# Distances' operand rows by block transposes and a trip through DRAM, with the aggregation one graph later

## Chip, cores, metric

The kernel runs on one core of a Trainium2 chip. The metric is the device time of one execution in microseconds; the time of record is the median over several runs.

## The reference, cut to what matters

There are 64 graphs of 256 nodes with 256 features. Layer 0 normalises an adjacency matrix and applies it and a weight matrix; a residual and a layer norm follow. Layer 1 has three branches that start from its result `x`: a convolution over the nodes, a message branch with distances, and a gated unit that joins them.

```python
# layer 1, message branch
s    = x @ w_se.T + b_se                       # 3 numbers for each node
sq   = sum(s * s, -1)
dist = sq[:, :, None] + sq[:, None, :] - 2 * einsum('bnd,bmd->bnm', s, s)
A    = exp(-dist) * mask                        # mask: the adjacency matrix given to the kernel's layer
msg  = relu(x @ w_msg.T + b_msg)
x_nmp = einsum('bnm,bmd->bnd', A, msg)          # the aggregation
x_in = concatenate([x_conv, x_nmp], -1)         # the gated unit's input
```

All data and arithmetic are float32.

## The kernel before

**Stages.** The graphs go in four groups of 16 (`Q`). For each group every graph passes `layer0` (from the adjacency matrix to `x1`) and `layer1` (first convolution, distances, messages, aggregation, and a small Fourier transform of the first convolution's output into the tile `V`). When 16 graphs are in `V`, the group's second convolution is done in the frequency domain: `products` multiplies `V` by the weights' transforms `u`, which are loaded from DRAM through six buffers, and `complex_end` transforms back and stores `xc_d`. Then `gates` runs the gated unit graph by graph: it loads what `layer1` stored (`xn_d`), `x1` and `xc_d`, multiplies by `wall` into `p_g`, and writes the output. Stages are overlapped: graphs 0 to 15 run beside the making of the weights' transforms (`weights`, matmuls `p_u`), the next 12 beside the first group's products and back transform, and later graphs beside the gates of the group before.

**Order.** Each stage is a Python generator that stops at `yield`; the functions `graphs`, `paced`, `merge` and `take` say which generator goes on next, and instructions are then put on the engines by a scheduler that may move a ready instruction ahead of one that it expects to wait. Each engine works off its own list strictly in order. SP issues nearly all loads in order, too: while it waits for a buffer or for data, later loads stand behind.

In `graphs` one graph's `layer1` is cut in seven pieces. `PLACES` says after which piece a piece of `layer0` (for two graphs ahead) or of the other work follows; `STATS` and `APPLIED` say where the last parts of a `layer0` (its layer norm's statistics, then the scaling) are taken up:

```python
PLACES = (("other",), ("layer0",), (), (), ("layer0",), ("other", "layer0"), ())
STATS, APPLIED = len(PLACES) - 1, 2
```

**The distances.** `p_conv` (L446) gives 256 features and the three columns of `s` for each chunk of 128 nodes. ScalarE copies the features to `h` and the three columns, four times over, into the constant tile `scols` (L450), where ones and zeros stand already; VectorE adds the halves of the negated squares (L454 to L457). TensorE turns the two chunks of `scols` with the identity (L495, into `p_rows`), ScalarE copies 64 of the rows to `dist_l` (L497) and VectorE the other 64 to `dist_r` (L499). A matmul over 32 rows for each chunk then gives `p_dist` (L506), ScalarE takes its Exp into `aT` (L507), and VectorE multiplies by the adjacency matrix (L508). The aggregation `p_nmp` (L515) follows in the next piece; ScalarE copies its result into `xn` (L519) and issues the store of `xn` to `xn_d` (L520).

The pieces of `layer1` are, in this order: `x1T` (turning `x1`, L429, into `xn`), `p_conv` with the columns, `p_msg`, `p_dft`, `p_rows`, `p_dist` with Exp and product, `p_nmp` with the store. For 12 graphs (`ALONE`) the turning of the next graph's `x1` stands just ahead of `p_nmp`.

**Buffers.** `xn` has two, `msg` and `aT` one each, `dist_l` and `dist_r` one each; `ps` is a pool of four PSUM banks that all of these products share.

Of the kernel before, what the change touches and what calls it, by code (L numbers as in the profile page):

```python
# [9 lines left out]
F32 = mybir.dt.float32  # L10
AF = mybir.ActivationFunctionType
ALU = mybir.AluOpType
AX = mybir.AxisListType

P = 128
# [11 lines left out]
def kernel(  # L27
# [44 lines left out]
    const = ctx.enter_context(tc.tile_pool(name="const", bufs=1))  # L72
    dram = ctx.enter_context(tc.tile_pool(name="dram", bufs=1, space=bass.MemoryType.DRAM))
# [4 lines left out]
    work = ctx.enter_context(tc.tile_pool(name="work", bufs=2))  # L78
# [3 lines left out]
    def bank(name):  # L82
        return ps.tile([P, 512], F32, tag="bank", name=name)
# [7 lines left out]
    def mark(op, gates=0):  # L91
        marks.append((op.ins, gates))
# [43 lines left out]
    ident = const.tile([P, P], F32)  # L136
# [8 lines left out]
    nc.vector.tensor_scalar(alpha_t, alpha_t, MIN_ALPHA, None, op0=ALU.max)  # L145


    scols = const.tile([P, NCH, P], F32, name="scols")
    nc.gpsimd.memset(scols, 0.0)
    for c in (NSE, 32 + NSE):  # L150
        nc.gpsimd.memset(scols[:, :, c : c + 1], 1.0)

# [187 lines left out]
    xn_d = [dram.tile([P, 2 * DCH, N], F32, name=f"xn_d{g}") for g in range(B)]  # L340
    XN = {}
    ALONE = set()
# [80 lines left out]
    def x1_transposed(g):  # L423
        x1 = X1.pop(g)
        xn = XN[g] = work.tile([P, 2 * DCH, N], F32, name="xn")
        p = bank("p_x1T").rearrange("p (k n) -> p k n", k=DCH)
        for k in range(DCH):
            for c in range(NCH):
                nc.tensor.transpose(p[:, k, c * P : (c + 1) * P], x1[:, c, k * P : (k + 1) * P], ident)  # L429
        nc.vector.tensor_scalar(xn[:, 0], p[:, 0], others_only, unit, op0=ALU.mult, op1=ALU.add)  # L430
        nc.scalar.copy(xn[:, 2 * DCH - 1], p[:, 1])

    def layer1(g, place):

        if g not in XN:
            x1_transposed(g)
        xn, adjT = XN.pop(g), ADJT.pop(g)
        x1T = xn[:, 0 : 2 * DCH : 2 * DCH - 1]
        yield

        h = work.tile([P, NCH, D], F32, name="h", bufs=1)
        cols = scols.rearrange("p c (q r) -> p c q r", r=32)
        for c in range(NCH):
            p = bank("p_conv1")[:, : D + NSE]
            for k in range(DCH):
                nc.tensor.matmul(  # L446
                    p, x1T[:, k, c * P : (c + 1) * P], wc1[:, k, :], start=k == 0, stop=k == DCH - 1
                )
            nc.scalar.activation(h[:, c, :], p[:, :D], AF.Relu)
            nc.scalar.copy(cols[:, c, :, :NSE], p[:, D:].unsqueeze(1).to_broadcast([P, 4, NSE]))  # L450

        s3 = cols[:, :, 0, :NSE]
        sq3 = small.tile([P, NCH, NSE], F32, name="sq3")
        nc.vector.scalar_tensor_tensor(sq3, s3, -1.0, s3, op0=ALU.mult, op1=ALU.mult)  # L454
        nsq = small.tile([P, NCH], F32, name="nsq")
        nc.vector.tensor_reduce(nsq, sq3, AX.X, ALU.add)
        last = nc.vector.tensor_scalar(  # L457
            cols[:, :, 2:4, NSE], nsq.unsqueeze(2).to_broadcast([P, NCH, 2]), 0.5, None, op0=ALU.mult
        )
        mark(last)  # L460
        mark(last)
        yield
        msg = work.tile([P, NCH, D], F32, name="msg", bufs=1)
        p = bank("p_msg").rearrange("p (c d) -> p c d", c=NCH)
        for c in range(NCH):
            for k in range(DCH):
                nc.tensor.matmul(  # L467
                    p[:, c, :], x1T[:, k, c * P : (c + 1) * P], wmsg[:, k, :], start=k == 0, stop=k == DCH - 1
                )
        mark(nc.scalar.activation(msg, p, AF.Relu))  # L470
        yield


        mid = GT // 2
        if TILES[0] is not V:
            AWAY.append(place)
        for k in range(DCH):
            p = bank("p_dft")

            for c, t0, t1 in ((0, 0, mid + 1), (1, mid - 1, GT)):  # L480
                first = t0 + 1 - c * mid
                nc.tensor.matmul(  # L482
                    p[:, t0 * FL : t1 * FL], h[:, c, k * P : (k + 1) * P],
                    fwd[:, first : first + t1 - t0, :].rearrange("p t f -> p (t f)"),
                    start=c == 0, stop=True, skip_group_check=c == 1,
                )
            nc.scalar.copy(
                TILES[0][:, :, k, place * GT : (place + 1) * GT],
                p[:, : GT * FL].rearrange("p (t f) -> p f t", f=FL),
            )  # L490

        yield
        p = bank("p_rows")
        for c in range(NCH):
            nc.tensor.transpose(p[:, c * P : (c + 1) * P], scols[:, c, :], ident)  # L495
        dl = work.tile([64, N], F32, name="dist_l", bufs=1)
        nc.scalar.copy(dl, p[0:64, :N])  # L497
        dr = work.tile([64, N], F32, name="dist_r", bufs=1)
        nc.vector.tensor_copy(dr, p[64:P, :N])  # L499
        yield  # L500

        aT = work.tile([P, NCH, 2, P], F32, name="aT", bufs=1)
        for c in range(NCH):
            rows = slice(32 * c, 32 * c + 32)
            p = bank("p_dist")[:, :N]
            nc.tensor.matmul(p, dl[rows, c * P : (c + 1) * P], dr[rows, :], start=True, stop=True)  # L506
            nc.scalar.activation(aT[:, c].rearrange("p n q -> p (n q)"), p, AF.Exp, bias=nsq[:, c : c + 1], scale=2.0)  # L507
        mark(nc.vector.tensor_mul(aT, aT, adjT[:, :, 0:3:2, :]))  # L508
        yield
        if g in ALONE:  # L510
            x1_transposed(g + 1)
        p = bank("p_nmp").rearrange("p (k n) -> p k n", k=DCH)
        for k in range(DCH):
            for mc in range(NCH):
                nc.tensor.matmul(  # L515
                    p[:, k, :], msg[:, mc, k * P : (k + 1) * P], aT[:, mc].rearrange("p n q -> p (n q)"),
                    start=mc == 0, stop=mc == NCH - 1,
                )
        nc.scalar.copy(xn[:, 1 : 1 + DCH], p)  # L519
        nc.scalar.dma_start(xn_d[g], xn)  # L520
        yield

# [412 lines left out]
    def chain(*stages):  # L935
        for stage in stages:
            yield from stage
# [13 lines left out]
    def run(stage):  # L951
        for _ in stage:
            pass
# [14 lines left out]
            yield  # L968


    PLACES = (("other",), ("layer0",), (), (), ("layer0",), ("other", "layer0"), ())
    STATS, APPLIED = len(PLACES) - 1, 2
    ENDS = [iter(())]

    def graphs(first, part, others):


        for i in part:
            load(first + i + 3)
# [12 lines left out]

    with tc.tile_pool(name="setup", bufs=1) as setup:
        load_taps(setup, 0)
# [85 lines left out]
    def copies(V2):  # L1080

        waiting = list(AWAY)
        AWAY.clear()
        TILES[0] = V
        for i in waiting:
            nc.scalar.copy(V[:, :, :, i * GT : (i + 1) * GT], V2[:, :, :, i * GT : (i + 1) * GT])
            yield

    late = nothing()
    for q in range(NQ):  # L1090
        first = (q + 1) * Q
        more = q + 1 < NQ
        end = chain(complex_end(q), copies(V2) if more else iter(()))
# [99 lines left out]
```

## Time and profile before

| | |
|---|---|
| median of 3 runs | 2127.64 us (2127.56 to 2128.44) |
| profiled execution | 2127.71 us, of which span 2125.9 us |
| mean granted TensorE clock | 0.988 |
| TensorE busy (matmuls) | 2006.1 us, 94% of the span |
| VectorE, ScalarE, GpSimd busy | 1474.1, 905.3, 666.8 us |
| DMA | 298.05 MB, mean 140 GB/s |
| `p_rows`: 128 transposes | 24.7 us busy |
| copies to `dist_l` (ScalarE) and `dist_r` (VectorE), 64 each | 23.4 and 27.2 us busy |
| `p_dist`: 256 passes | 46.2 us busy |
| `p_nmp`: 512 passes | 122.6 us busy |

How to read it: times are of one execution on the chip. A float32 matmul is recorded as two passes. Matmuls are pipelined and the recorded lengths overlap, so busy times are more than what an instruction holds back the next one by. PE is TensorE's matmuls, PEld its weight loads, DVE VectorE, ACT ScalarE, POOL GpSimd, SP the engine that only issues transfers. The span is the time from the first to the last instruction; the execution is 1.8 us longer.

### The profile page before, as it was taken

What the parts mean: (1) busy time and instruction counts of PE and PEld (TensorE: products, weight loads), DVE (VectorE), ACT (ScalarE), POOL (GpSimd) and SP (SyncE); (2) the same over time, 40 slices, a digit from 0 to 9 for tenths busy, and PEclk for the clock granted to TensorE, in tenths of its full rate; (3) what the DMA queues carried; (4) which work ended last, traced back from release to release, by engine and by line L of the source; (5) the groups of instructions that cost most, each with busy time, mean ns of one, the idle gap of its engine ahead of it and who ended that gap; (6) DMA issues with size and microseconds to landing.
All of it is one profiled execution on the core that took longest, in us unless ns stands there. A gap on an engine that the chain in (4) does not pass through costs nothing. (4 is left out here: it accounts for less than half of the span.)

```text
span 2125.9 us, 26260 instructions
## 1 busy us (share of the span) xinstructions
PE 2006.1 (94%) x8157; PEld 1443.2 (68%) x8157; DVE 1474.1 (69%) x3347; ACT 905.3 (43%) x2114; POOL 666.8 (31%) x672
## 2 busy tenths in 40 slices
PE   6999999888999999999999999999999999899997
PEld 5888788766667756667777666667777765555554
DVE  5555567775558788774556888875445889977776
ACT  4666643456432234555553123446554123233333
POOL 3445310121431243223321234323232123344443
PEclk9999999999999999999999999999999999999999
DMA  4766556433437645344335655334323754443331
GB/s 125 230 210 200 192 183 209 154 132 119 122 96 226 194 123 139 114 120 120 94 99 179 201 155 140 118 104 134 96 93 100 243 146 131 111 118 95 93 94 56
DMA packets 305289, 298.05 MB, mean 140 GB/s; under 512 B 84192, under 2 KB 283956, under 8 KB 305150
## 3 DMA queue, kind: packets, MB, share of 16 engines
q1 hardware_dynamic: 245198, 200.37, 32.1%
q10 hardware_dynamic: 44480, 67.39, 8.9%
q0 software_dynamic: 15472, 28.61, 6.0%
q8 instruction: 66, 1.08, 0.2%
q14 instruction: 73, 0.60, 0.1%
HBM read 193.19 MB, written 103.06 MB: 139 GB/s over the span
## 5 line engine op out<-in xcount | busy, mean ns | idle before, releaser
L856 PE MATMUL p_g<-wall,sums 128*128 128x384 f32 x1536 | 537.7, 489 | 11.6 <-DVE G L882 11.6
L856 PE MATMUL p_g<-wall,inputs 128*128 128x384 f32 x1152 | 409.4, 492 | 14.5 <-DVE G L874 14.1
L856 PEld LDWEIGHTS p_g<-wall,sums 128*128 128x128 f32 x1536 | 284.6, 191 | 200.3 <-issue 19.1
L856 PEld LDWEIGHTS p_g<-wall,inputs 128*128 128x128 f32 x1152 | 218.5, 192 | 167.5 <-DVE G L874 23.4
L838 POOL TENSOR_TENSOR sums<-inputs 128x384 f32<-128x384 f32 x128 | 139.9, 1093 | 343.2 <-PE p_g L856 296.9
L369 POOL TENSOR_TENSOR dis<-deg,neg_half 128x2 f32<-128x2 f32 x64 | 48.3, 754 | 475.7 <-DVE deg L367 468.6
L897 ACT ACTIVATE G<-G 128x512 f32<-128x512 f32 x128 | 80.7, 630 | 250.8 <-DVE G L884 148.6
L328 POOL TENSOR_TENSOR ln_rs<-ln_rs,neg_half 128x2 f32<-128x2 f32 x129 | 94.9, 736 | 275.1 <-DVE ln_rs L327 226.7
L541 PE MATMUL p_k<-u,VM 128*128 128x256 f32 x736 | 175.8, 381 | 4.1 <-DMA u<-ud 4.1
L541 PEld LDWEIGHTS p_k<-u,VM 128*128 128x128 f32 x736 | 139.4, 191 | 31.3 <-DMA u<-ud 3.9
L446 PE MATMUL p_conv<-wc,xn 128*128 128x259 f32 x512 | 130.4, 392 | 22.7 <-DVE xn L430 21.5
L399 PE MATMUL p_hT<-adjT,x 128*128 128x256 f32 x512 | 126.7, 391 | 15.6 <-ACT msg L470 8.2
L333 ACT ACTIVATE x_g<-x_g,ln_mr,ln_rs 128x256 f32<-128x256 f32 x128 | 70.0, 593 | 150.3 <-DVE ln_mr L331 148.3
L446 PEld LDWEIGHTS p_conv<-wc,xn 128*128 128x128 f32 x512 | 94.2, 191 | 53.1 <-DVE xn L430 31.1
L508 DVE TENSOR_TENSOR aT<-aT,adjT 128x512 f32<-128x512 f32 x64 | 44.8, 699 | 123.0 <-ACT aT L507 122.8
L409 PE MATMUL p_out<-w,hT 128*128 128x256 f32 x512 | 123.7, 384 | 3.4 <-ACT hT L404 3.0
L482 PE MATMUL p_dft<-fwd,h 128*128 128x240 f32 x512 | 117.4, 372 | 9.2 <-ACT scols L450 8.8
L515 PE MATMUL p_nmp<-aT,msg 128*128 128x256 f32 x512 | 122.6, 383 | 0.7 <-DVE aT L508 0.7
L467 PE MATMUL p_msg<-wmsg,xn 128*128 128x256 f32 x512 | 122.0, 381 | 0.0
L838 POOL TENSOR_TENSOR sums<-inputs,sums 128x384 f32<-128x384 f32 x64 | 70.2, 1097 | 161.3 <-PE p_g L856 160.6
L331 DVE SCALAR_TENSOR_TENSOR ln_mr<-ln_mv,ln_rs 128x2 f32<-128x2 f32 x129 | 47.3, 368 | 101.7 <-POOL ln_rs L328 101.7
L409 PEld LDWEIGHTS p_out<-w,hT 128*128 128x128 f32 x512 | 95.6, 190 | 29.9 <-ACT hT L404 9.9
(160 smaller groups left out, 3642.0 us busy)
## 6 DMA issues: line engine op xcount, KB each, us to landing
u<-ud SPq DMA_DIRECT2D x284, 256.0 KB
xn_d<-xn ACTq DMA_DIRECT2D x64, 512.0 KB
inputs<-xn_d SPq DMA_DIRECT2D x64, 512.0 KB
ud<-u_set POOLq DMA_DIRECT2D x39, 480.0 KB, 6.3
adj_t<-in_adj_dram SPq DMA_DIRECT2D x64, 256.0 KB
x_t<-in_x_dram SPq DMA_DIRECT2D x64, 256.0 KB
x_d<-x ACTq DMA_DIRECT2D x64, 256.0 KB
xc_d<-VM SPq DMA_DIRECT2D x64, 256.0 KB
```

The costliest lines, as they stand in the source:

```text
L328: nc.gpsimd.tensor_tensor(rs[:, : len(chunks)], rs[:, : len(chunks)], neg_half[:, : len(chunks)], op=ALU.pow)
L333: nc.scalar.activation(y[:, c, :], y[:, c, :], AF.Identity, bias=mr[:, c : c + 1], scale=rs[:, c : c + 1])
L399: nc.tensor.matmul(p[:, k, :], x1[:, mc, k * P : (k + 1) * P], adjT[:, mc, 1 - mc : 3 - mc, :].rearrange("p n q -> p (n q)"), start=mc == ...
L409: nc.tensor.matmul(p[:, c, :], hT[:, k, c * P : (c + 1) * P], w0[:, k, :], start=k == 0, stop=k == DCH - 1)
L446: nc.tensor.matmul(p, x1T[:, k, c * P : (c + 1) * P], wc1[:, k, :], start=k == 0, stop=k == DCH - 1)
L467: nc.tensor.matmul(p[:, c, :], x1T[:, k, c * P : (c + 1) * P], wmsg[:, k, :], start=k == 0, stop=k == DCH - 1)
L482: nc.tensor.matmul(p[:, t0 * FL : t1 * FL], h[:, c, k * P : (k + 1) * P], fwd[:, first : first + t1 - t0, :].rearrange("p t f -> p (t f)") ...
L515: nc.tensor.matmul(p[:, k, :], msg[:, mc, k * P : (k + 1) * P], aT[:, mc].rearrange("p n q -> p (n q)"), start=mc == 0, stop=mc == NCH - 1,)
L541: nc.tensor.matmul(p[:, j * D : (j + 1) * D], v[:, k, :], u[:, k, :], start=k == 0, stop=k == DCH - 1)
L838: nc.gpsimd.tensor_tensor(S[i], x, y, op=op)
L856: nc.tensor.matmul(p[:, : 3 * HD] if k == 0 else p[:, HD:], a[:, k], wall[:, b, k].rearrange("p t d -> p (t d)"), start=first and k == 0, ...
L897: nc.scalar.activation(rz, rz, AF.Tanh, scale=0.5)
```

## The change

`scols` shrinks from 128 to 32 columns a chunk and holds two groups of four (three columns of `s` and one more) instead of four groups of 32. VectorE turns it in blocks of 32x32 into a new tile `tr`. SP stores `tr` to one of four small DRAM tensors `sd`, and loads from there, with four transfers, the four rows of each chunk that the distances need: `dist_r` with all 256 nodes (in an order by blocks) and `dist_l` with the chunk's 128. TensorE's two transposes, `p_rows` and both copies out of it are gone. The distance matmuls take four rows instead of 32, and the Exp reads PSUM in the blocks' order.

The aggregation leaves the end of its own graph: the graph's tiles are put in `PENDING`, and `aggregated()` runs one graph later, between `p_conv` and `p_msg`, and once more at the end of each run of `graphs`. In the 12 graphs alone, the turning of the next graph's `x1` now stands ahead of `p_dist`. `PLACES`, `STATS` and `APPLIED` are set to the new pieces.

```diff
-    scols = const.tile([P, NCH, P], F32, name="scols")
+    RB4 = NSE + 1
+    scols = const.tile([P, NCH, 32], F32, name="scols")
     nc.gpsimd.memset(scols, 0.0)
-    for c in (NSE, 32 + NSE):
-        nc.gpsimd.memset(scols[:, :, c : c + 1], 1.0)
+    nc.gpsimd.memset(scols[:, :, NSE : NSE + 1], 1.0)
+    sd = [dram.tile([P, NCH * 32], F32, name=f"sd{i}") for i in range(4)]
...
-        cols = scols.rearrange("p c (q r) -> p c q r", r=32)
+        cols = scols[:, :, : 2 * RB4].rearrange("p c (q r) -> p c q r", r=RB4)
...
-            nc.scalar.copy(cols[:, c, :, :NSE], p[:, D:].unsqueeze(1).to_broadcast([P, 4, NSE]))
+            nc.scalar.copy(cols[:, c, :, :NSE], p[:, D:].unsqueeze(1).to_broadcast([P, 2, NSE]))
...
-        last = nc.vector.tensor_scalar(
-            cols[:, :, 2:4, NSE], nsq.unsqueeze(2).to_broadcast([P, NCH, 2]), 0.5, None, op0=ALU.mult
-        )
+        nc.vector.tensor_scalar(cols[:, :, 1, NSE], nsq, 0.5, None, op0=ALU.mult)
+        tr = work.tile([P, NCH * 32], F32, name="tr")
+        last = nc.vector.transpose(tr, scols.rearrange("p c i -> p (c i)"))
+        dl = work.tile([64, P], F32, name="dist_l")
+        dr = work.tile([64, N], F32, name="dist_r")
+        nc.sync.dma_start(sd[g % 4], tr)
+        across = sd[g % 4].rearrange("(b r) x -> r b x", r=32)
+        for c in range(NCH):
+            rows = slice(32 * c, 32 * c + RB4)
+            nc.sync.dma_start(dr[rows].rearrange("r (b x) -> r b x", b=4), across[RB4 : 2 * RB4])
+            nc.sync.dma_start(dl[rows].rearrange("r (b x) -> r b x", b=4), across[:RB4, :, 32 * c : 32 * c + 32])
         mark(last)
         mark(last)
+        yield
+        aggregated()
         yield
...
-        p = bank("p_rows")
-        for c in range(NCH):
-            nc.tensor.transpose(p[:, c * P : (c + 1) * P], scols[:, c, :], ident)
-        dl = work.tile([64, N], F32, name="dist_l", bufs=1)
-        nc.scalar.copy(dl, p[0:64, :N])
-        dr = work.tile([64, N], F32, name="dist_r", bufs=1)
-        nc.vector.tensor_copy(dr, p[64:P, :N])
-        yield
-
+        yield
+
+        if g in ALONE:
+            x1_transposed(g + 1)
         aT = work.tile([P, NCH, 2, P], F32, name="aT", bufs=1)
         for c in range(NCH):
-            rows = slice(32 * c, 32 * c + 32)
+            rows = slice(32 * c, 32 * c + RB4)
             p = bank("p_dist")[:, :N]
-            nc.tensor.matmul(p, dl[rows, c * P : (c + 1) * P], dr[rows, :], start=True, stop=True)
-            nc.scalar.activation(aT[:, c].rearrange("p n q -> p (n q)"), p, AF.Exp, bias=nsq[:, c : c + 1], scale=2.0)
+            nc.tensor.matmul(p, dl[rows], dr[rows], start=True, stop=True)
+            nc.scalar.activation(
+                aT[:, c].rearrange("p n (b i) -> p n b i", i=32), p.rearrange("p (b n i) -> p n b i", n=NCH, i=32),
+                AF.Exp, bias=nsq[:, c : c + 1], scale=2.0,
+            )
         mark(nc.vector.tensor_mul(aT, aT, adjT[:, :, 0:3:2, :]))
-        yield
-        if g in ALONE:
-            x1_transposed(g + 1)
-        p = bank("p_nmp").rearrange("p (k n) -> p k n", k=DCH)
-        ...
-        nc.scalar.copy(xn[:, 1 : 1 + DCH], p)
-        nc.scalar.dma_start(xn_d[g], xn)
-        yield
+        PENDING.append((g, xn, msg, aT))
+        yield
+
+    def aggregated():
+        while PENDING:
+            g, xn, msg, aT = PENDING.pop()
+            p = bank("p_nmp").rearrange("p (k n) -> p k n", k=DCH)
+            ...
+            nc.scalar.copy(xn[:, 1 : 1 + DCH], p)
+            nc.scalar.dma_start(xn_d[g], xn)
...
-    PLACES = (("other",), ("layer0",), (), (), ("layer0",), ("other", "layer0"), ())
-    STATS, APPLIED = len(PLACES) - 1, 2
+    PLACES = (("other",), ("layer0",), (), (), (), ("layer0",), ("other", "layer0"))
+    STATS, APPLIED = 1, 3
     ENDS = [iter(())]
...
             for piece, _ in enumerate(layer1(first + i, i)):
-                if piece == APPLIED:
-                    run(ENDS.pop())
-                    ENDS.append(given["layer0"])
-                elif piece == STATS:
-                    next(given["layer0"], "end")
+                if piece == STATS:
+                    next(ENDS[0], "end")
+                elif piece == APPLIED:
+                    run(ENDS[0])
+                    ENDS[0] = given["layer0"]
...
             yield from given["other"]
+        aggregated()
```

The statistics of a `layer0` are so taken up in the next graph's second piece, where before they came in the last piece of the same graph.

More of the change, by code (lines that the diff above doesn't have):

```diff
@@ L492, in layer1 @@
         yield
-        p = bank("p_rows")
-        for c in range(NCH):
-            nc.tensor.transpose(p[:, c * P : (c + 1) * P], scols[:, c, :], ident)
-        dl = work.tile([64, N], F32, name="dist_l", bufs=1)
-        nc.scalar.copy(dl, p[0:64, :N])
-        dr = work.tile([64, N], F32, name="dist_r", bufs=1)
-        nc.vector.tensor_copy(dr, p[64:P, :N])
-        yield
-        aT = work.tile([P, NCH, 2, P], F32, name="aT", bufs=1)
-        for c in range(NCH):
-            rows = slice(32 * c, 32 * c + 32)
-            p = bank("p_dist")[:, :N]
-            nc.tensor.matmul(p, dl[rows, c * P : (c + 1) * P], dr[rows, :], start=True, stop=True)
-            nc.scalar.activation(aT[:, c].rearrange("p n q -> p (n q)"), p, AF.Exp, bias=nsq[:, c : c + 1], scale=2.0)
-        mark(nc.vector.tensor_mul(aT, aT, adjT[:, :, 0:3:2, :]))
         yield
@@ L511, in layer1 @@
             x1_transposed(g + 1)
-        p = bank("p_nmp").rearrange("p (k n) -> p k n", k=DCH)
[L513 to L518, printed above, removed]
-        nc.scalar.copy(xn[:, 1 : 1 + DCH], p)
-        nc.scalar.dma_start(xn_d[g], xn)
-        yield
+        aT = work.tile([P, NCH, 2, P], F32, name="aT", bufs=1)
+        for c in range(NCH):
+            rows = slice(32 * c, 32 * c + RB4)
+            p = bank("p_dist")[:, :N]
+            nc.tensor.matmul(p, dl[rows], dr[rows], start=True, stop=True)
[3 more added lines that the diff above has]
+            )
+        mark(nc.vector.tensor_mul(aT, aT, adjT[:, :, 0:3:2, :]))
+        PENDING.append((g, xn, msg, aT))
+        yield
+    PENDING = []
+    def aggregated():
+        while PENDING:
+            g, xn, msg, aT = PENDING.pop()
+            p = bank("p_nmp").rearrange("p (k n) -> p k n", k=DCH)
+            for k in range(DCH):
+                for mc in range(NCH):
+                    nc.tensor.matmul(
+                        p[:, k, :], msg[:, mc, k * P : (k + 1) * P], aT[:, mc].rearrange("p n q -> p (n q)"),
+                        start=mc == 0, stop=mc == NCH - 1,
+                    )
+            nc.scalar.copy(xn[:, 1 : 1 + DCH], p)
+            nc.scalar.dma_start(xn_d[g], xn)
     VM = freq.tile([P, FL, D], F32, name="VM")
```

## The prediction

> **What bounds the kernel now.** I read the page's busy times first, then busy time by stage, then TensorE's order in time, then its waits.
>
> The busy line, and three 50 us stages (columns: stage, length, busy us of PE, PEld, DVE, ACT, POOL with instruction counts, granted clock, DMA share, GB/s):
>
> ```profile
> PE 2006.1 (94%) x8157; PEld 1443.2 (68%) x8157; DVE 1474.1 (69%) x3347; ACT 905.3 (43%) x2114; POOL 666.8 (31%) x672
> ```
> ```profile
> 130.00:180.00 50.00, 50.00 (x251) 42.26 (x250) 27.06 (x65) 32.51 (x83) 24.73 (x25) 1.00 0.63 205
> 450.00:500.00 50.00, 42.88 (x210) 34.13 (x210) 38.73 (x108) 27.08 (x74) 9.07 (x9) 1.00 0.30 102
> 1000.00:1050.00 50.00, 48.59 (x213) 36.28 (x212) 25.53 (x71) 26.09 (x66) 17.55 (x18) 1.00 0.41 126
> ```
>
> TensorE is the bound. In the first stage (graphs 0 to 12 beside the weights' transforms, 80 to 230 us) it is never idle; in the stage of graphs alone (450 to 500) it lacks 7 us in 50, and with gates mixed in 1 to 3. So a PE instruction removed is worth its time in the first stage, and a new wait of PE costs its length there.
>
> TensorE's order in time (start, length, instruction):
>
> ```profile
> 167.04 1.78 PE L482 MATMUL p_dft<-fwd,h 128*128 128x240 f32 x8
> 168.66 0.38 PE L495 MATMUL p_rows<-ident,scols 128*128 128x128 f32 x2
> 168.88 1.89 PE L399 MATMUL p_hT<-adjT,x 128*128 128x256 f32 x8
> 170.70 0.70 PE L506 MATMUL p_dist<-dist_r,dist_l 32*128 32x256 f32 x4
> 171.33 1.99 PE L307 MATMUL p_u<-taps,dft_w 85*120 85x256 f32 x8
> ```
>
> The lengths overlap; the price is from start to start. The two transposes of `p_rows` cost 168.88 - 168.66 = 0.22 us, not the 0.38 shown. In the same way eight passes of 256 columns (four matmuls) cost 1.73 (`p_msg`, 165.31 to 167.04), `p_dft` 1.62, four transposes 0.44 (160.96 to 161.40), `p_dist` 0.63, and three matmuls of `p_g` 1.94.
>
> TensorE's waits that touch the edit (us in total, times, longest):
>
> ```profile
> PE p_conv L446 <- DVE xn L430: 21.5, 19, 3.1
> PE p_dist L506 <- DVE dist_r L499: 4.1, 8, 1.1
> PE p_rows L495 <- DVE ln_mv L326: 3.2, 2, 1.6
> PE p_rows L495 <- DVE scols L457: 2.7, 4, 0.9
> PE p_rows L495 <- ACT x L333: 0.5, 1, 0.5
> PE p_hT L399 <- ACT dist_l L497: 1.3, 2, 0.6
> ```
>
> **What goes.** Transposes: 64 x 0.22 = 14.1 us of PE. The waits of `p_rows`, of `p_dist` for `dist_r`, and of `p_hT` for `dist_l`: 3.2 + 2.7 + 0.5 + 4.1 + 1.3 = 11.8 us. The copy on ACT (64 x 0.366 = 23.4) and on VectorE (64 x 0.426 = 27.2) go too; I count nothing for them, since neither is the bound. The new block transpose takes VectorE some of that back: the trace's transpose of 128x512 took 702 ns and its smallest operations about 160, so 128x64 lies between 0.16 and 0.70; I take 0.2, near the small end because it has an eighth of the elements.
>
> **What stays.** `p_dist` keeps its 256 columns; four rows instead of 32 shorten nothing that a row shows. Its two halves are parted by other matmuls in 46 of the 64 graphs in the new order. Four passes of 128 rows cost half of 1.73, 0.87, against 0.63 here, so the parting costs 0 to 46 x 0.24 = 11 us; I take 0. The Exp of 128x256 reads PSUM in runs of 32; copies with equally broken views (L487) cost no more per element than plain ones, so 0.
>
> **The moved aggregation.** Eight passes of `p_nmp`, ACT's copy (0.58 us) and the issue of the 512 KB store of `xn` (0.34) go from the end of graph g to just behind `p_conv` of graph g + 1. `p_nmp` waited 0.7 us in all for its operand, so nothing is won there; the work is moved into the stretch that must now cover the transfers. On ACT the copy stands ahead of the ReLU of `msg`, with 1.7 us of `p_msg` to cover it. The store frees `xn` a graph later: issued about 3 us behind `p_conv`, 3.5 us long in the chain, it is in by about 6.5, and the next write of that buffer comes no earlier than about 7.9 where `x1T` is early; 1.4 us to spare, cost 0. In the stage of graphs alone, `x1T` now stands ahead of `p_dist` and `p_out` (0.63 + 1.73 us) instead of ahead of `p_nmp` (1.73), and VectorE takes `xn` before `p_out`'s epilogue. Of the 21.5 us of `p_conv` waits, some 17 lie between 200 and 640 us; bounds 0 and 17, I take 8.
>
> **The new wait.** `p_dist` now needs: VectorE's chain after `p_conv`, the block transpose, a store, and loads issued only when the store has landed. The first part is in the trace:
>
> ```profile
> 163.12 1.92 PE L446 MATMUL p_conv<-wc,xn 128*128 128x259 f32 x8
> ...
> 167.09 0.17 DVE L457 TENSOR_SCALAR scols<-nsq 128x4 f32<-128x4 f32 x1
> ```
>
> That is 2.2 us from the end of `p_conv` (165.04) to the end of L457 (167.26). Over the 64 graphs this distance X was 1.08 at best, 2.2 in the median, over 3 in 20 of them. For one transfer the nearest rows are small loads:
>
> ```profile
> 2007.59 0.55 SPq L790 DMA_DIRECT2D inputs<-x_d  x1
> 2010.43 1.67 POOL L813 TENSOR_TENSOR inputs<-inputs 128x512 f32<-128x512 f32 x1 [3.19 <-DMA inputs<-x_d]
> ```
> ```profile
> wc<-in_b_se_dram POOLq DMA_DIRECT2D x1, 0.0 KB, 2.4
> wmsg<-in_b_msg_dram POOLq DMA_DIRECT2D x1, 1.0 KB, 2.1
> ```
>
> The first is 2.8 us from issue to user, with 0.55 of issue for 256 pieces; SP's small issues took about 0.28 (0.28 and 0.25 at 2.18 and 2.50 us of the span). So a hop costs 2.1 to 3.4 (the slowest L790 case, 1518.0 to 1521.4); I take 2.4, nearest to the small pieces. Then the operands of the first `p_dist` are there X + 0.3 + 2.4 + 2.4 + 0.28 = X + 5.4 after `p_conv`, those of the second 0.56 later.
>
> Against it stands the cover on PE in the new order: `p_adjT` 0.44, `p_nmp` 1.73, `p_msg` 1.73, `p_dft` 1.62, `p_hT` 1.73 = 7.25 us; `x1T` adds 0.44 where graphs run alone, each `p_u` 0.43, each `p_g` matmul 0.65. Cover is 7.25 or less in 22 graphs, up to 8 in 12, 8 to 8.6 in 17, more in 13. Taking each graph's X against its own cover (for graph 28 without the 6.1 us that `p_dft` itself waits), the waits sum over 64 graphs to 10 us at 2.1 a hop, 19 at 2.4, 32 at 2.7, 58 at 3.0 and 101 at 3.4. I take 19; 15 of it falls in graphs 28 to 63, where X is uneven.
>
> In the first stage three stores of 480 KB a graph (median landing 6.3 us) go out just when the new store does, at a DMA share of 0.6 to 0.75. Two hops that share engines with them may each be a us slower: 13 graphs, 0 to 2.5 us each, 0 to 32; I take 4, since `p_u` lengthens the cover there to 8.5.
>
> A page of the Trainium skill speaks against this change: DMA: Bandwidth & Descriptors, section "Anatomy of one DMA", says that a transfer of any size pays a nearly constant 2 us, most of it the receipt from the memory written, DRAM's being the longest. By it a hop is an estimated 2.1 us and the sum would be about 10 us lower than mine; the 2.8 us row is slower than the rule.
>
> **SP's queue.** Five issues of about 0.28 us a graph, and two waits in order: for the transpose, then for the store's landing. Behind them stand loads of `adj`, `x`, the gates' inputs, stores of `xc` and the loads of `u`. The first four are wanted a graph later. Loads of `u` are six deep (5.2 us of products); in graphs 16 to 19 the new order puts the store behind loads that themselves wait for products after `p_conv`, so SP would stand there anyway. 0 to 3 us in each of four graphs; I take 0.
>
> **Sum.** -14.1 - 11.8 - 8 + 19 + 4 = -11 us. The profiled execution took 2127.71 (span 2125.9), the median is 2127.64, so no correction: 2117 us.
>
> **Rivals.**
> - **Slow hops** (slower). If a hop under load costs 3.0 or more, PE waits 58 us or more, and 2127.7 - 34 + 58 + 10 = 2162. It decides from about 2.7 a hop, where 32 cancels the gain. For: the L790 rows of 2.8 to 3.4, the DMA share, loads queued ahead of the small ones. Against: those rows hold 0.55 us of issue and 256 scattered words. Chance 0.34.
> - **Gain swallowed.** Where PE idles anyway, freed PE time turns into the next wait (`G` for `p_g`, 25.7 us in all); only the first 16 graphs gain 16 x 0.22 = 3.5, and the new waits eat it: 2122 to 2131. For: PE lacks 7 us in 50 in the middle stage. Against: the gates' stages are 97% busy. Chance 0.14.
> - **SP held**: `u` late by 3 us in four graphs on top of the forecast's waits at 2.7 a hop: about 2138. Chance 0.04.
> - **Forecast**, hops of 2.1 to 2.6: 2094 to 2123. Chance 0.48.
>
> **The numbers.** A measurement here tells about 0.2% from no change, 4.3 us. Faster: 0.45 of the forecast's 0.48 and 0.05 of the swallowed gain, 0.50. Same: 0.03 + 0.03 of slow hops near the balance + 0.07 = 0.13. Slower: 0.31 + 0.02 + 0.04 = 0.37. The range, 2098 to 2162, reaches from all `p_conv` waits gone with hops of 2.1 up to hops of 3.0; the forecast case alone is 2098 to 2123.
>
> **What would show it.** Right: no `p_rows`; `p_dist` waiting for DMA `dist_r` or `dist_l` about 20 us in all, mostly behind 500 us; `p_conv` waits for `xn` falling below 15. Wrong: `p_dist` waits of 50 us or more, or spread over the first 230 us (then the stores of `ud` are the reason), or `p_k` waiting for `u` well over its 5.1 us.

## The result, and the profile after

| | before | after |
|---|---|---|
| median | 2128.04 us (2127.56 to 2129.88, 4 runs) | 2278.44 us (2267.23 to 2294.82, 4 runs) |
| profiled execution | 2127.71 us, span 2125.9 | 2279.28 us, span 2277.2 |
| mean granted TensorE clock | 0.988 | 0.954 |

The ratio is 1.0711, 95% interval 1.0645 to 1.0777: 7% slower, where 2117 us was forecast and 2162 was the upper end.

The page's busy line of the changed kernel, then three 50 us stages at about the places of those shown of before (columns as there; the eighth group is the granted clock):

```profile
PE 2092.4 (92%) x8029; PEld 1483.3 (65%) x8029; DVE 1444.1 (63%) x3347; ACT 897.5 (39%) x2050; POOL 663.8 (29%) x671
```
```profile
130.00:180.00 50.00, 42.00 (x177) 32.49 (x175) 16.69 (x40) 23.02 (x55) 14.26 (x14) 0.90 0.49 142
550.00:600.00 50.00, 44.42 (x208) 36.34 (x207) 36.05 (x120) 26.81 (x73) 9.82 (x10) 0.97 0.35 114
1110.00:1160.00 50.00, 46.75 (x183) 34.03 (x182) 19.94 (x60) 25.46 (x63) 12.04 (x13) 0.92 0.36 108
```

TensorE has 128 instructions fewer and is busy 86.3 us longer; its idle time grew from 119.8 to 184.8 us (span less busy). The 151.3 us of the span are these two parts, 86.3 + 65.0. The longer busy time has two parts of its own: a lower clock, and `p_dist`. Its two halves now stand apart, with other matmuls between them, in 46 of the 64 graphs (2 before), and its busy time went from 46.2 to 90.2 us. A graph at full clock and without a wait shows the price of that:

```profile
1084.85 0.69 PE L512 MATMUL p_dist<-dist_r,dist_l 4*128 4x256 f32 x2
1085.48 0.91 PE L870 MATMUL p_g<-wall,sums 128*128 128x384 f32 x2
1086.32 0.69 PE L512 MATMUL p_dist<-dist_r,dist_l 4*128 4x256 f32 x2
1086.94 1.99 PE L410 MATMUL p_out<-w,hT 128*128 128x256 f32 x8
```

From start to start each half costs 0.63 and 0.62 us; together they cost 0.63 before (170.70 to 171.33). An estimate from these rows is 46 x 0.62 = 28 us at full clock for the 46 graphs.

The stage from 30 us to the first product of the first group, before and after, shows the idle time and the lower clock at their largest:

```profile
30.00:282.70 252.70, 245.28 (x1204) 204.65 (x1205) 135.18 (x330) 155.84 (x406) 105.58 (x99) 0.99 0.61 192
```
```profile
30.00:383.60 353.60, 295.98 (x1154) 228.20 (x1154) 130.42 (x326) 154.83 (x384) 104.94 (x99) 0.84 0.48 139
```

Idle time went from 7.4 to 57.6 us there, busy time from 245.28 to 295.98, the clock from 0.99 to 0.84. Of the added busy time, 17.7 us are `p_dist`'s (11.2 before, 28.9 after, partly at the lower clock).

TensorE's waits after (us in total, times, longest), whole span and then 30 to 383 us alone:

```profile
PE p_dist L512 <- DMA dist_l<-sd: 60.2, 30, 5.8
PE p_conv L447 <- DVE xn L431: 17.5, 8, 3.0
PE p_hT L400 <- DVE tr L460: 5.1, 2, 2.6
PE p_k L555 <- DMA u<-ud: 3.9, 4, 1.6
```
```profile
PE p_dist L512 <- DMA dist_l<-sd: 38.1, 11, 5.8
```

The new wait is 60.2 us, 38.1 of it in the first stage. Another 5.3 us there are one wait of `p_u` at 49.5 us, which the kernel before doesn't have. Graph 6 shows what one such wait is made of (start, length, instruction; rows of VectorE, GpSimd, SP and TensorE picked from the timeline):

```profile
167.16 1.99 PE L447 MATMUL p_conv<-wc,xn 128*128 128x259 f32 x8
...
168.57 2.92 POOL L314 TENSOR_TENSOR u_set<-u_set,u_set 120x1024 f32<-120x1024 f32 x1
...
172.11 0.59 POOL L316 DMA_DIRECT2D ud<-u_set  x1
172.19 0.16 DVE L332 SCALAR_TENSOR_TENSOR ln_mr<-ln_mv,ln_rs 128x2 f32<-128x2 f32 x1 [2.92 <-POOL ln_rs L329]
172.27 1.76 DVE L455 SCALAR_TENSOR_TENSOR sq<-scols 128x6 f32<-128x6 f32 x1
...
174.50 0.25 DVE L460 STREAM_TRANSPOSE tr<-scols 128x64 f32<-128x64 f32 x1
```
```profile
174.77 0.36 SPq L463 DMA_DIRECT2D sd<-tr  x1
175.24 1.12 SPq L108 DMA_DIRECT2D adj_t<-in_adj_dram  x1
176.41 2.59 SPq L291 DMA_DIRECT2D taps<-in_conv2T_dram  x1
180.24 0.27 SPq L467 DMA_DIRECT2D dist_r<-sd  x1
```
```profile
182.63 1.19 PE L512 MATMUL p_dist<-dist_r,dist_l 4*128 4x256 f32 x2 [4.24 <-DMA dist_l<-sd]
183.74 2.06 PE L308 MATMUL p_u<-taps,dft_w 85*120 85x256 f32 x4
185.73 1.22 PE L512 MATMUL p_dist<-dist_r,dist_l 4*128 4x256 f32 x2
186.88 3.78 PE L410 MATMUL p_out<-w,hT 128*128 128x256 f32 x8
```

`p_conv` ends at 169.1. VectorE is ready with the block transpose only at 174.75, 5.6 us later: it waits 2.92 us for a small GpSimd operation behind the sum of `u_set`, and soon after L455 takes 1.76 us (the like operation of before 0.17 in the median). The store goes out at 174.77 while two stores of `ud` run, and the first load only at 180.24, 5.5 us later: SP spends 3.7 us of that on issuing two other loads, and then still waits 1.2 us for the store's landing. The loads are quick: the first `p_dist` starts 2.1 us after the issue of the second one, which it needs. It starts at 182.6, 13.5 us after `p_conv`. And then `p_out` lasts 3.78 us, not its usual 1.99. The windows around it say why (same columns):

```profile
177.00:182.00 5.00, 1.38 (x7) 0.84 (x5) 0.00 (x0) 1.17 (x2) 0.00 (x0) 1.00 0.80 246
182.00:187.00 5.00, 4.37 (x9) 2.24 (x9) 0.00 (x0) 1.07 (x3) 0.52 (x1) 0.53 0.23 61
187.00:192.00 5.00, 5.00 (x14) 4.07 (x15) 1.94 (x4) 1.37 (x5) 0.00 (x0) 0.50 0.34 93
192.00:197.00 5.00, 5.00 (x25) 4.23 (x25) 2.47 (x9) 3.03 (x9) 3.61 (x2) 0.94 0.25 57
```

After 4.24 us without work TensorE runs at half its clock. In half-microsecond windows the clock stands at 0.50 from 182.5 to 192.5, ten us in which five us of work are lost. So one wait is paid about twice. Graphs 5 to 10 all look like this and take 23 to 27 us each, where before took 16.

### The profile page after: what moved, and what is told of

It is laid out like the page before. It is cut to its first block, busy times and chain, and to the rows that moved or that the text cites. A ratio compares the mean times of both kernels' runs of the same rounds, so it can differ in the third digit from the quotient of the medians.

```text
span 2277.2 us, 26624 instructions
## 1 busy us (share of the span) xinstructions
PE 2092.4 (92%) x8029; PEld 1483.3 (65%) x8029; DVE 1444.1 (63%) x3347; ACT 897.5 (39%) x2050; POOL 663.8 (29%) x671
## 3 DMA queue, kind: packets, MB, share of 16 engines
q1 hardware_dynamic: 259534, 203.26, 30.7%
## 4 chain that ended last, share of the span: by engine, by line
PE 38%; DVE 21%; DMA 5%; issue 5%; POOL 3%; ACT 3%; SPq 1%; ACTq 0%; POOLq 0%; DVEq 0%
PE p_g L870 22%; PE p_k L555 5%; PE p_out L410 3%; PE p_dist L512 2%; PE p_hT L400 2%; DMA sd<-tr 1%; DMA dist_l<-sd 1%; DVE ln_st L326 1%; POOL ln_rs L329 1%; DVE VM L742 1%; PE p_nmp L530 1%; DVE VM L605 1%; PE p_dft L493 1%; DVE VM L606 1%; DVE G L923 1%
## 5 line engine op out<-in xcount | busy, mean ns | idle before, releaser
L870 PE MATMUL p_g<-wall,sums 128*128 128x384 f32 x1536 | 546.1, 493 | 13.4 <-DVE G L896 13.3
L870 PE MATMUL p_g<-wall,inputs 128*128 128x384 f32 x1152 | 418.0, 498 | 24.5 <-DVE G L888 19.6
L870 PEld LDWEIGHTS p_g<-wall,inputs 128*128 128x128 f32 x1152 | 219.3, 194 | 180.0 <-DVE G L888 30.7
L410 PE MATMUL p_out<-w,hT 128*128 128x256 f32 x512 | 152.4, 450 | 0.7 <-ACT hT L405 0.7
L512 PE MATMUL p_dist<-dist_r,dist_l 4*128 4x256 f32 x256 | 90.2, 478 | 63.2 <-DMA dist_l<-sd 60.2
L410 PEld LDWEIGHTS p_out<-w,hT 128*128 128x128 f32 x512 | 111.9, 225 | 40.6 <-issue 12.3
L400 PEld LDWEIGHTS p_hT<-adjT,x 128*128 128x128 f32 x512 | 99.4, 198 | 44.1 <-ACT x L392 6.4
```

Source lines behind the costliest of these rows:

```text
L400: nc.tensor.matmul(p[:, k, :], x1[:, mc, k * P : (k + 1) * P], adjT[:, mc, 1 - mc : 3 - mc, :].rearrange("p n q -> p (n q)"), start=mc == ...
L410: nc.tensor.matmul(p[:, c, :], hT[:, k, c * P : (c + 1) * P], w0[:, k, :], start=k == 0, stop=k == DCH - 1)
L512: nc.tensor.matmul(p, dl[rows], dr[rows], start=True, stop=True)
L870: nc.tensor.matmul(p[:, : 3 * HD] if k == 0 else p[:, HD:], a[:, k], wall[:, b, k].rearrange("p t d -> p (t d)"), start=first and k == 0, ...
```

## The experiments

The theory at the start: the trip through DRAM arrives too late, TensorE idles, and the idling costs clock on top. Its rivals: the new order costs by itself; SP's extra transfers cost whoever waits for them; the clock falls for another reason; the operands are late for VectorE's sake and not for the transfers'.

To compare kernels by stage I took from each trace the time at which VectorE completes `scols` for a graph, and subtracted that of before. Gain or loss of each stretch in us (the last column is the difference of the whole span):

| kernel | to graph 15 | 15 to 27 | 27 to 32 | 32 to 63 | rest | span |
|---|---|---|---|---|---|---|
| after | +103.3 | -8.7 | +11.6 | +43.4 | +1.6 | +151.3 |
| 1 order alone | +18.5 | -6.9 | +2.9 | -5.4 | -1.0 | +8.1 |
| 2 trip alone | +74.1 | +2.2 | +10.9 | +18.4 | +0.9 | +106.4 |
| 3 no dependence | +31.7 | -10.9 | +0.7 | -10.8 | -4.7 | +6.0 |
| 4 one `ud` store | +47.6 | -7.9 | +7.2 | +34.2 | -2.6 | +78.4 |
| 5 matmuls in the wait | +92.2 | -8.0 | +10.0 | +44.3 | +3.3 | +141.7 |
| 6 distances later | +40.2 | -6.3 | +9.2 | -16.6 | 0.0 | +26.5 |
| 8 mixed | +3.0 | -9.3 | +9.4 | -13.9 | +3.5 | -7.3 |

The graphs with a parted `p_dist`, and its busy time, differ too: 46 and 90.2 us in after, 0 and 46.0 in 1, 39 and 84.0 in 2, 10 and 55.5 in 3, 46 and 82.2 in 4, 43 and 81.7 in 5, 15 and 57.0 in 6, 3 and 46.9 in 8. No experiment changes the parting by itself.

The runs of the kernel before had medians of 2128.0 to 2130.1 us beside these kernels; ratios are to the runs on the same chip.

**1. The order alone.** After's pieces and later aggregation, with the transposes on TensorE put back in the piece that the trip left empty.

```diff
+        p = bank("p_rows")
+        for c in range(NCH):
+            nc.tensor.transpose(p[:, c * P : (c + 1) * P], scols[:, c, :], ident)
...
-        nc.sync.dma_start(sd[g % 4], tr)
...
```

> The aggregation one graph later and the new pieces as in the changed kernel, but the operand rows still by TensorE's two transposes (no trip through DRAM). Theory A (the trip's waits, and TensorE's clock falling behind them, are the whole loss): no wait of p_dist for a DMA, granted clock 0.98 or more, 2110 to 2130 us. Rival B (the new order itself costs in the gates' stages, where 56 us of the loss lies): 2150 to 2190 us. Rival C (the order gains what the prediction claimed, about 8 us of p_conv's waits): 2115 to 2122 us, graphs alone 4 to 8 us shorter.

Measured: 2140.76 us, ratio 1.0042 (1.0025 to 1.0059), clock 0.987. The loss of 150 us isn't in the order. The order costs 18.5 us in the first stage and wins 6.9 among the graphs alone; B falls, C holds only there, and A's total is missed by 11 us, since A gave the order no price.

**2. The trip alone.** The order of before, with the transposes replaced by the trip.

> The trip through DRAM as in the changed kernel, but the aggregation and the pieces as before, so that p_nmp (1.73 us) does not lie between p_conv and p_dist. Theory A: the waits grow by up to 1.7 us a graph and the clock falls further: 2350 to 2450 us, granted clock 0.92 or less. Rival B (the later aggregation costs, not the trip): under 2250 us.

Measured: 2234.59 us, ratio 1.0477 (1.0451 to 1.0503). My expectation missed: I had looked only at the cover, which is 1.73 us shorter, and this kernel is 44 us faster than the whole change. B's number is met, but the trip by itself still costs 106 us. In its first stage `p_dist` waits only 8.0 us for transfers; `p_conv` waits 15.0 for `xn`, `p_nmp` 6.7 for `aT` and `p_u` 5.4 for `taps`, so that pricing `p_dist`'s wait alone misses most of the trip's cost there. In its trace the block transpose ends 2.16 us after `p_conv` in graphs 1 to 12 (4.14 in after), and the store takes 2.70 us until SP issues the first load (4.64 in after). The later aggregation bought 1.73 us of cover and lost more: in its order VectorE's chain comes later, and the store falls together with those of `ud`.

**3. All transfers, no dependence.** The four loads read the tensor that the graph before stored.

```diff
-        across = sd[g % 4].rearrange("(b r) x -> r b x", r=32)
+        across = sd[max(g - 1, 0) % 4].rearrange("(b r) x -> r b x", r=32)
...
-                AF.Exp, bias=nsq[:, c : c + 1], scale=2.0,
+                AF.Exp, bias=nsq[:, c : c + 1], scale=0.0,
```

> The changed kernel with all its transfers, but the four loads read the small DRAM tensor of the graph before, so that they don't wait for this graph's store; the Exp's scale is 0, so that its result is finite (values of the aggregation are so left out of what the kernel computes). Theory A: no long waits of p_dist, granted clock 0.98 or more, 2090 to 2115 us. Rival D (five more issues a graph on SP and their traffic hold back loads and stores, whoever waits): 2150 us or more with p_dist's waits gone, and other DMA waits grown.

Measured: 2134.17 us, ratio 1.0014 (1.0000 to 1.0029), clock 0.983. All five transfers are there, and 144 of the 150 us are gone: the dependence on this graph's operands is the loss, not the traffic. The dependence brings more than the wait, for without it `p_dist` is parted in 10 graphs instead of 46, an estimated 36 x 0.62 = 22 us at full clock. From graph 15 on this kernel is 25.7 us shorter than before, 21.0 of it up to graph 63, where distances are made; I had put 34 us for all 64 graphs. A's total is missed because the first stage stays 31.7 us longer. Two groups of it there, for VectorE the product and for TensorE the wait:

```profile
L517 DVE TENSOR_TENSOR aT<-aT,adjT 128x512 f32<-128x512 f32 x15 | 29.7, 1981 | 29.9 <-ACT aT L513 29.9
```
```profile
PE p_conv L447 <- DVE xn L431: 19.3, 13, 3.0
```

The product took 692 ns in that stage before; here up to 2.84 us, where it stands beside GpSimd's sum of `u_set`. That pair is experiment 7.

**4. Fewer stores of `ud`.** One of three in each of the first 13 graphs.

```diff
-                for d, u in zip(ud, (us[0], us[3], us[2])):
+                for d, u in zip(ud, (us[0],)):
...
-            u, ud[i][n * GC : (n + 1) * GC].rearrange("c g o -> (c g) o")[:D].rearrange("(k p) o -> p k o", p=P)
+            u, ud[0][n * GC : (n + 1) * GC].rearrange("c g o -> (c g) o")[:D].rearrange("(k p) o -> p k o", p=P)
```

> The changed kernel with one of the three 480 KB stores of ud in each of the first 13 graphs; the products read that one for all three (two of the three transforms are left out of the result). Theory A1 (the hops of the first stage are slow because ud's stores share the DMA engines): hops there 2.5 to 3 us, p_dist's waits in the first 16 graphs from 38 to 15 us or less, that stage from 351 to 270 to 300 us, total 2200 to 2230 us. Rival A2 (the wait comes from VectorE's late chain and SP's other issues ahead of the loads): the stage stays above 335 us, total above 2260 us.

Measured: 2213.33 us, ratio 1.0385 (1.0321 to 1.0449). TensorE's wait there:

```profile
PE p_dist L512 <- DMA dist_l<-sd: 4.3, 4, 2.2
```

From 38.1 to 4.3 us. From the store's issue to the first load it is now 1.93 us in graphs 1 to 12, 4.64 in after; VectorE's distance is as long as in after (4.01). A1 holds for the cause, and its total of 2200 to 2230 us too: 56 us of the loss, in the first stage, come from the stores of `ud` beside the trip. Whether they slow the small store in the DMA engines or otherwise, the run doesn't tell; SP's issues between store and loads became short as well (0.4 to 0.5 us each in graphs 5 to 10, 1.1 to 2.6 in after). Another 9 us lie in graphs 32 to 63, which the edit doesn't touch; executions of after alone spread over 28 us.

**5. Matmuls in the wait.** Eight matmuls that nobody reads ahead of `p_dist` in 16 graphs.

```diff
+        if g < 16:
+            p = bank("p_warm")[:, :N]
+            for i in range(8):
+                nc.tensor.matmul(p, ident, wmsg[:, 0, :], start=i == 0, stop=i == 7)
```

> The changed kernel with eight matmuls more (256 columns each, 3.46 us at full clock) ahead of p_dist in graphs 0 to 15; nothing reads their result. They add 16 x 3.46 = 55 us of TensorE's work and end no transfer sooner. Theory K (TensorE's clock falls because it idles some us before p_dist, and the slow matmuls behind it cost as much again as the wait): TensorE doesn't idle there, granted clock of the first stage from 0.84 to 0.95 or more, that stage from 351 to 310 to 330 us, total 2235 to 2260 us: more work, and a shorter time. Rival L (the clock falls for another reason, such as load or DMA, and the wait alone is the loss): clock 0.86 or less, the added work shows in full where it is longer than the waits, total 2290 to 2320 us.

Measured: 2271.30 us, ratio 1.0643 (1.0600 to 1.0686). The first stage and the added group:

```profile
30.00:373.00 343.00, 316.06 (x1406) 256.90 (x1407) 144.48 (x326) 153.04 (x384) 105.33 (x99) 0.95 0.46 144
```
```profile
L511 PE MATMUL p_warm<-wmsg,ident 128*128 128x256 f32 x256 | 57.9, 379 | 0.0
```

57.9 us more work, and the stage is 11 us shorter up to the point where as many instructions of its own have run (its first product starts at 377.8, 6 us earlier than in after). Without the added group TensorE is busy 316.06 - 57.9 = 258.2 us, 37.8 less than in after for as much work: most of the clock's price there goes when TensorE is kept at work. Idle time fell by 30.7. L falls. The whole kernel's gain of 7 us on after lies within the spread of after's executions; clear of it is only that 57.9 us more work didn't make the kernel longer. The total lies between the two expectations, above K's: `p_conv`'s waits for `xn` rose from 8.4 to 20.5 us in that stage, which I had not allowed for.

**6. Distances a graph later too.** `p_dist`, Exp and product of graph g stand ahead of `p_conv` of graph g + 1 (in `distances`). `msg` has two buffers here, `dist_l` and `dist_r` one each.

```diff
     def layer1(g, place):
+        distances()
         if g not in XN:
             x1_transposed(g)
...
-        aggregated()
-        yield
-        msg = work.tile([P, NCH, D], F32, name="msg", bufs=1)
+        msg = work.tile([P, NCH, D], F32, name="msg")
...
         mark(nc.scalar.activation(msg, p, AF.Relu))
         yield
+        aggregated()
```

> Trip through DRAM for every graph, with the distances a graph later too: p_dist, Exp and product of graph g stand ahead of p_conv of graph g + 1, its aggregation behind p_msg of graph g + 1 (msg in two buffers). The trip has 10 us or more of cover on TensorE. Theory A (the waits and what follows them are the loss): no wait of p_dist for a DMA beyond 5 us in all, granted clock 0.98 or more, 2105 to 2140 us; graphs 16 to 63 take 15 to 25 us less than before. Rival D (the queue of SP and the order cost by themselves): 2150 us or more.

Measured: 2153.91 us, ratio 1.0108 (1.0092 to 1.0125). `p_dist` waits 4.6 us for transfers in the whole span, as the theory has it, and from graph 15 on the kernel is 13.7 us shorter than before, just short of the theory's 15 to 25. The total meets D's number instead: 40.2 us are lost in the first stage and 9.2 between graphs 27 and 32. The first stage has 15 us more idle time (one wait of `p_u` of 6.1 us, 4.6 for the trip, the rest small), a clock of 0.93, and 12 of its graphs with a parted `p_dist`, busy 9.4 us longer. Neither theory foresaw that split.

**7. GpSimd's sum on VectorE**, in the kernel of experiment 3.

```diff
-                nc.gpsimd.tensor_tensor(us[2], us[0], us[1], op=ALU.add)
+                nc.vector.tensor_add(us[2], us[0], us[1])
```

> As the kernel that reads the operands of the graph before (Exp's scale 0, values left out), and the sum of u_set (1024 elements a partition, 2.9 to 3.3 us on GpSimd in each of 13 graphs) on VectorE, where its like took 1.2 us. Theory M (in the new order the product aT falls beside GpSimd's sum and waits it out: 2.84 us in place of 0.69, so that VectorE turns x1 late and p_conv waits): the product back at 0.7 us, first stage from 282 to 250 to 262 us, total 2103 to 2115 us. Rival N (the first stage of that kernel is late because SP's small transfers hold taps and x back): the stage stays above 272 us, total 2125 us or more.

Measured: 2116.49 us, ratio 0.9935 (0.9911 to 0.9959). The product is back at 0.684 us, `p_conv` waits 5.0 us instead of 19.3 there, and the first stage lost 16.2 us instead of 31.7. The total is just above M's range: M holds for half of that stage's loss, and what is left is about what the order costs by itself (18.5, experiment 1).

**8. A mixed kernel.** Graphs 0 to 15 as before; from graph 16 on the trip with distances and aggregation a graph later, as in experiment 6.

```diff
+            old = first + i < Q
+            for piece, _ in enumerate((layer1_first if old else layer1)(first + i, i)):
...
+                for name in (PLACES_FIRST if old else PLACES)[piece]:
```

> Graphs 0 to 15 in the order of before and with TensorE's transposes; graphs 16 to 63 by the trip through DRAM, distances and aggregation a graph later as in the run above (tr and diagonal in one buffer for space). Theory A: first stage as before (250 us), from graph 16 on no DMA waits of p_dist and 64 - 16 = 48 graphs without transposes: 15 to 25 us gained, 2103 to 2115 us, faster than before. Rival P (TensorE's freed time turns into other waits outside the first stage too, so nothing is gained): 2122 to 2140 us.

Measured: 2122.05 us, ratio 0.9966 (0.9949 to 0.9982): faster than both kernels, by 0.34% than before. The first stage is as before and stays so; from graph 16 on TensorE waits for none of the trip's transfers. The gain, 7 us, is less than half of what I expected: 9 us come back as a loss between graphs 27 and 32, where `p_g` has one new wait for GpSimd (4.5 us) and `p_nmp` waits 2.0 us. From the first product on, `p_out` waits 8.8 us for ScalarE (2.2 before), `p_nmp` 7.6 for VectorE (0.7) and `p_hT` 8.1 for `adjT` (4.6), while `p_hT`'s 8.2 for `msg` are gone. P's total is met and A's isn't, but the kernel is faster than before, as A has it.

**9. The changed kernel with the sum on VectorE**, same edit as in 7.

> The changed kernel with the sum of u_set in the first 13 graphs on VectorE (1.22 us there) in place of GpSimd (2.9 to 3.3 us). Theory M (in the new order VectorE's small operations behind p_conv stand beside GpSimd's sum and are late: the distance from p_conv's end to the block transpose is 4.1 us there, against 2.2 taken): this distance falls to 2.0 to 2.6 us, the operands come 1.5 to 2 us sooner, p_dist's waits in the first stage from 38 to 10 to 18 us, that stage from 351 to 295 to 320 us, total 2215 to 2245 us. Rival H (the hops under ud's stores are the whole of it): stage above 335 us, total above 2258 us.

Measured: 2268.43 us, ratio 1.0640 (1.0614 to 1.0667). H's numbers are met, and M falls for this kernel:

```profile
PE p_dist L512 <- DMA dist_l<-sd: 41.7, 10, 6.6
```

VectorE's distance in graphs 1 to 12 goes from 4.14 to 3.65 us only, and the store's time from 4.64 to 5.59, so that nothing is won for `p_dist`.

**10 to 12. The same edit elsewhere**: in the kernel of 6, in the kernel before, in the mixed kernel.

> Distances and aggregation a graph later, no transpose on TensorE in any graph, and the sum of u_set on VectorE. Theory M: the first stage, 40 us longer than before in the run without this edit, comes within 8 to 20 us of before; total 2115 to 2135 us. Rival H: the stage stays 30 us longer or more, total 2142 us or more.

> The kernel before with the sum of u_set on VectorE: a control. In the old order only one small operation of VectorE (1.01 us in place of 0.16) meets the sum and p_conv waits 5 us in that stage, so both theories expect 2121 to 2131 us, at most 6 us less than before.

> The mixed kernel (graphs 0 to 15 as before, the others by the trip with distances and aggregation a graph later) with the sum of u_set on VectorE: as the mixed kernel less what the control gains, 2113 to 2126 us, faster than before by 0.2 to 0.7%.

Measured: 2146.93 us (1.0075, 1.0058 to 1.0092), 2147.04 us (1.0073, 1.0045 to 1.0102) and 2136.71 us (1.0031, 1.0015 to 1.0047). Experiment 10 meets H's number, and its first stage stays 34.5 us longer. The control and the mixed kernel miss: the edit makes the kernel before 0.7% slower, `p_conv` waiting for `xn` 14.4 us instead of 5.2 in the first stage. So the sum's place is worth something only in one order and costs in another. The mixed kernel is best without it. Why the control loses was not followed up.

## Why the prediction was wrong

**The step that failed is the new wait, in two terms and one omission.** I had 19 us for it and 4 more for the first stage. It is 60.2 us of waits, and behind them most of the 86.3 us of longer busy time (an estimate: 28 us for the parting of `p_dist`, less 14 for the transposes, leave some 72 for the lower clock); 144 us lie between the kernel that waits and the one that doesn't (experiment 3). A term outside the wait failed too, the parting of `p_dist`.

- **The first stage's extra, 4 us (bounds 0 and 32).** Measured 38.1 us of waits in that stage. I let both hops together be up to 2.5 us a graph slower beside the stores of `ud`. In graphs 5 to 10 the store's hop alone took 5.5 to 6.2 us against the 2.4 of the sum, so 3.1 to 3.8 more. The load's hop was near the sum: 1.4 to 3.1 us from the issue of the second load to the first `p_dist`. Experiment 4 shows the stores of `ud` as the cause. The text named the sign to look for, waits over 50 us and spread over the first 230, and both came.
- **X, VectorE's chain.** I took each graph's X from the trace before, 2.2 us in the median. But the change moves other work on VectorE and GpSimd too: with the block transpose it was 4.14 us on average in graphs 1 to 12, against 2.07 + 0.3 forecast. Without the block transpose X was 3.8 in after there, and 3.8 in experiment 1 as well, which has the order and no trip. In graphs 28 to 63 it was 4.1 against 3.1 + 0.3. In the gates' stages the hops were as forecast (2.3 to 2.6 us), and the wait there was 21.4 us against 15 forecast; this term was near.
- **The clock, left out.** I priced a us of waiting at a us. In the stretch to 383 us, 50.2 us of added idle time came with 50.7 us of added busy time. About 9 us of the latter are the parting of 14 graphs at full clock, the rest goes with the clock of 0.84, and experiment 5 ties most of it to the idling. From the first product of the first group on, 15 us of added idle time came with 36 us of added busy time; there `p_dist` alone is busy 26 us longer, in 32 parted graphs. The trace of before held a small case, which I read past: `p_out` of 2.47 us behind an idle 2.23. The Trainium skill, in TensorE: Matmul & The Clock Gate, section "Part 1: The HAM clock gate (the "warmup" mystery)", says that a window of about 3.4 us of idleness halves the clock, and about 3.4 us of sustained work restores it. The first half agrees with the 4.24 us here but not with the 2.23; the second does not agree, since half clock lasted 10.0 us.
- **The parting of `p_dist`, 0 us (bounds 0 and 11).** The 46 graphs came as forecast, the price didn't: I set four passes of 128 rows at 0.87 against 0.63, so 0.24 a graph. The rows show 0.63 + 0.62 against 0.63, so 0.62 a graph and 28 us.

**The gains were near.** Transposes and their waits were put at 14.1 + 11.8 + 8 = 34 us for 64 graphs; without the dependence the graphs from 15 to 63 gain 21.0. In the first stage nothing was left of it: the new order costs 18.5 us there, a step that I had put at nothing, and the product beside GpSimd's sum most of the rest (15.5 us, experiment 7). On the latter the Trainium skill, SBUF — State Buffer, section "SBUF: two separate sides", says that VectorE's operations with two inputs and GpSimd's lock one port pair for a whole instruction; 2.84 us for a product of 0.69 beside a sum of 3.38 agrees.

**What held.** The block transpose took 0.20 to 0.25 us (0.2 forecast). The loads of `u` behind SP's new waits cost nothing: `p_k` waited 3.9 us, 5.1 before. `p_conv`'s waits fell, by 4 us instead of 8. The section of the Trainium skill that the prediction names (in DMA: Bandwidth & Descriptors) describes transfers issued through GpSimd, while the trip's go out on SP; the 5.5 to 6.2 us here, and 1.5 us for the same store in graphs 5 to 7 of experiment 4, lie on both sides of its nearly constant 2 us. Its figure also spoke for the change, not against it: shorter hops made the forecast sum better.

**The rival** "slow hops" named the right side and a part of the mechanism. It had 0.34 and a price that stopped at 3.0 us a hop with nothing for the clock, so 2162 us; the 2117 us were the wrong choice between two cases whose deciding number, the hop beside heavy stores, no row of the trace showed.

**Still open**: what each part of the 40 us costs that experiment 6 loses in the first stage, where 4.6 us are waited for the trip; why the order puts VectorE's chain later; and why moving the sum slows the kernel before.

## What to carry to other kernels

A dependent trip through DRAM needs cover for the worst stretch of traffic, not for the median row. The one kernel with a working trip that gained here (experiment 8) gave it a whole iteration and kept it out of the stage that stores most; the whole iteration alone (6) still lost 1.1%. A wait of 4 to 6 us on a busy TensorE cost about twice its length here, for the clock fell behind it. Two short matmuls that stand together can be cheaper than the same two with other work between (0.63 against 1.25 us here), so read such a price from start to start in both arrangements. And when an edit moves the order of work, the lead times read from the old trace no longer hold; read them anew on each engine that feeds the new chain.

## What the runs showed of the hardware

- An idle 4.24 us was followed by 10.0 us at half clock; in the trace of before, an idle 2.23 us already stretched the next `p_out` to 2.47 us.
- A 32 KB store beside two 480 KB stores took 5.5 to 6.2 us until its reader could be issued (graphs 5 to 10), 1.93 us on average when two of three such stores were gone (graphs 1 to 12).
- Two halves of `p_dist` (two passes of 256 columns each) cost 0.63 us together, and 0.63 and 0.62 us when other matmuls stood between them, at a granted clock of 1.00.
- Issuing is not of one price: one load of `taps` (L291) took SP 2.59 us at 176.41, and four of them 1.80 us in all at 181.58.
- Filling a wait with matmuls that nobody reads shortened the stage by 11 us although it added 57.9 us of work.
